# A recurrence with a mixture of experts behind it: second bias, slot stores, loads and steps rearranged in layer 0

## The chip, the cores and the metric

The kernel runs on one core of one Trainium2 chip. The metric is the device time of one execution in microseconds (us). Three timed runs and one profiled execution of the kernel before are at hand; the profile also gives each instruction's start and end on the five engines (PE is TensorE, DVE is VectorE, ACT is ScalarE, POOL is GpSimd, SP is the queue engine that issues loads), the DMA transfers, and the TensorE clock that was granted.

## The reference

The input x has 8 sequences of 512 tokens of width 256, all in float32. Two layers follow one another. Only layer 0 is touched by the change:

```python
h = layernorm(x) * (1 + ca) + sa
# attention: 16 heads of width 16, a delta rule along the tokens
q, k = l2_normalize(silu(h @ Wq.T)), l2_normalize(silu(h @ Wk.T))
v, beta = silu(h @ Wv.T), sigmoid(h @ Wbeta.T)
for t in range(512):                       # M is 16x16 for each sequence and head
    out_t = q_t @ M
    delta = v_t - M @ k_t
    M = M + beta_t * outer(k_t, delta)
x = x + ga * ((out / rms(out)) * rms_weight) @ Wo.T
h = layernorm(x) * (1 + cb) + sb
# experts: each token goes to the one of 8 experts with the largest gate logit
for e in range(8):
    y = relu(h @ w1[e] + b1[e]) @ w2[e] + b2[e]     # 256 -> 1024 -> 256
    out = out + (top_idx == e) * y
x = x + gb * out
```

Layer 1 is softmax attention with a relative position bias and a dense mixture of eight 256x256 experts. Its code is the same before and after.

## The kernel before, in words

Layer 0 takes the 512 tokens as four tiles of 128 tokens, i = 0 to 3; each tile holds the 128 tokens of all 8 sequences (b = 0 to 7). The recurrence of a tile is `scan(i)`: 128 steps on VectorE, each of six instructions (L760 to L794: the products with the key, their sum, the update and the next delta). Its state M is 128x256 and is carried from tile to tile, so the four scans can only follow one another. They run from 56 to 1007 us of the profiled execution.

Everything else of layer 0 is cut into *pieces*. A piece is a function with a number, the step of the scan behind which it is to be issued. The loop that places them is this:

```python
for s, step in enumerate(steps or ()):
    while left and left[0][0] <= s:
        with tc.issue_after(step):
            left.pop(0)[1]()
```

The numbers set the program order. The framework's scheduler then orders the instructions of each engine by their estimated times within what `issue_after` and the buffers allow. During `scan(i)` the pieces are:

- `front(i + 1)`: the next tile's normalized Q, K, V. For each pair p of sequences, `stats(p)` issues the load of `xt` (two buffers) on SP and has ScalarE sum it and take the deviation `sda` (L525); `normal(p)` has VectorE invert it (`rsa`, L541, L542). For each sequence b, `turn`, `project` and `squares` run on ScalarE, TensorE and GpSimd, then `roots` and `scales` normalize; `heads` lays out K and V for the next scan. The front begins at step 47 (for tile 1 at step 30). After the last load SP writes zeros over the slot array `hs_d`.
- `follow(i - 1)`: what comes after the recurrence of the tile before. Its `attend` computes the attention output of that tile from Q, K and the deltas on TensorE: for each sequence `turn`, `scores`, `mask` (`pair`, L891), `weigh` (L924 is the new part of the state), `state` (`dm`, L970; `bdM`, L967), `project`; then `roots` (`ms`, L974), `rest` (adds the output to `x1`) and `stats` of the second layernorm. Its pieces lie on steps 0 to about 65. Then `route` picks the experts and forms the slots.
- `experts(i - 1)`: the tile's 1024 tokens are scattered by an indirect DMA of GpSimd into 15 slots of 128 rows, each slot with one expert. For each slot j SP loads its rows `hslot`, GpSimd fetches the expert's weights by two indirect DMAs (`w0` 128x2056 and `w1` 128x2304, two buffers each; L1192), TensorE multiplies twice (L1238 and L1259) with ScalarE's activation between (L1247), and the sum `py` gets the second bias and is stored to `ys_d`:

```python
nc.scalar.copy(ysb, py[:, :D])
nc.gpsimd.tensor_add(ysb, ysb, w[:, NFC * D :])
nc.gpsimd.dma_start(rows, ysb)
```

 The fetch of `w0` for slot j + 2 is issued behind these on GpSimd. The last slot of the last tile is the exception: VectorE adds the bias to `py`, and SP stores it. Of tiles 0 and 1, eleven slots are issued during the scan and four during the next; of tile 2, twelve during scan 3 and three behind it; of tile 3, all behind it.
- the gathers: when a tile's slots are stored, GpSimd gathers the rows back (L1284), multiplies them by the gates (L1319) and adds them to x in memory by an accumulating DMA (L1320). Those of tile 2 fall behind the scans, between the slots of tile 3. For tile 3 VectorE multiplies.

Behind the scans come `attend(3)`, its routing, the last slots and the gathers, up to about 1270 us. Layer 1 begins at 1287 us.

Of the kernel before, what the change touches and what calls it, by code (L numbers as in the profile page):

```python
# [19 lines left out]
P = 128  # L20
B = 8
S = 512
D = 256
# [41 lines left out]
def tile_two_layers(ctx: ExitStack, tc: tile.TileContext, t: dict, out: bass.AP):  # L65
# [223 lines left out]
    with ExitStack() as l0:  # L289
# [183 lines left out]
        def front(i, at):  # L473
# [27 lines left out]
                    zero.unsqueeze(1).to_broadcast([P, 2 * NSLOT, P]),  # L501
                )

            def stats(p):
                xt = ep.tile([P, 2, D], F32, tag="xt", name=f"xt{i}_{p}", bufs=2)
                load = nc.sync.dma_start(
                    xt,
                    t["x"][2 * p : 2 * p + 2, i * P : (i + 1) * P, :].rearrange("b p d -> p b d"),
                )
                mv = ep.tile([P, 2, 2], F32, tag="mva", name=f"mva{i}_{p}", bufs=2)  # L510
# [13 lines left out]
                sd = ep.tile([P, 2], F32, tag="sda", name=f"sda{i}_{p}")  # L524
                nc.scalar.activation(sd, mv[:, :, 1], AF.Sqrt, bias=ln_eps, scale=1.0 / D)  # L525
                got[p] = xt, mv, sd
                if p == B // 2 - 1:

                    with tc.issue_after(load.ins):
                        nc.sync.dma_start(  # L530
                            hs_d[i].rearrange("(p j) (c d) -> p (j c) d", p=P, c=2),
                            zero.unsqueeze(1).to_broadcast([P, 2 * NSLOT, P]),
                        )

            def normal(p):
                xt, mv, sd = got[p]
# [179 lines left out]
            if i == 0:  # L716
                pieces.append((0, stats_first))
                for b in range(B):
                    pieces.append((4 * b + 4, lambda b=b: turn_first(b)))

                    pieces.append((4 * b + 9, lambda b=b: project_first(b)))
                    pieces.append((4 * b + 13, lambda b=b: squares_first(b)))
                    later.append((1 + 2 * b, lambda b=b: project_q(b)))
                    later.append((4 + 2 * b, lambda b=b: squares_q(b)))
                pieces += [(46, roots_first), (47, scales_first)]
                later += [(22, roots_q), (25, scales_q)]
            else:
                for b in range(B):
                    p, c = divmod(b, 2)
                    if c == 0:  # L730
                        pieces.append((at + 8 * p, lambda p=p: stats(p)))
                        pieces.append((at + 8 * p + 6, lambda p=p: normal(p)))
                    pieces.append((at + 8 * p + 3 * c + 6, lambda b=b: turn(b)))
                    pieces.append((at + 8 * p + 3 * c + 7, lambda b=b: project(b)))
                    pieces.append((at + 8 * p + 3 * c + 13, lambda b=b: squares(b)))
                for h in range(B // n):

                    last = at + 16 * h + 32
                    pieces.append((last, lambda h=h: roots(h)))
                    pieces.append((last + 2, lambda h=h: scales(h)))  # L740
            turns = at + (55 if i else 48)
            pieces.append((turns, lambda: heads("K", qk[:, 1], 1.0)))
            pieces.append((turns + 3, lambda: heads("V", v, -1.0)))
            got["qk"] = qk
# [61 lines left out]
        def attend(i, qk, V, x1, norms):  # L806
# [166 lines left out]
            def roots(h):  # L973
                nc.vector.reciprocal(got["ms", h], got["ms", h])  # L974
# [207 lines left out]
        def experts(i, slot, idx, scatter):  # L1182
# [46 lines left out]
            for j in range(NSLOT):  # L1229
# [34 lines left out]
                rows = ys_d[i][j * P : (j + 1) * P, :]  # L1264
                if (i, j) == (NT - 1, NSLOT - 1):

                    nc.vector.tensor_add(ysb, py[:, :D], w[:, NFC * D :])
                    nc.sync.dma_start(rows, ysb)
                else:
                    nc.scalar.copy(ysb, py[:, :D])  # L1270
                    nc.gpsimd.tensor_add(ysb, ysb, w[:, NFC * D :])
                    nc.gpsimd.dma_start(rows, ysb)
# [36 lines left out]
            for b in range(B + DEPTH[i]):  # L1309
                if b < B:  # L1310

                    room = w1["fetched" if i < NT - 2 else "rows"]
                    yr = room[:, b * D : (b + 1) * D]
                    with tc.issue_after(issued["fetch"]):
                        gather(b, yr)
                    queue.append(yr)
                if b >= DEPTH[i]:
                    yr, k = queue.pop(0), b - DEPTH[i]
                    nc.gpsimd.tensor_mul(yr, yr, gates[1][:, k, :])  # L1319
                    nc.gpsimd.dma_start(x2d[k][i], yr, accum_op=ALU.add)  # L1320
                yield

# [103 lines left out]
        for i in range(NT):  # L1426
# [450 lines left out]
```

## Time and profile before

| | |
|---|---|
| three timed runs | 2044.92, 2048.03, 2048.41 us, median 2048.03 |
| profiled execution | 2056.27 us, span 2054.6 us |
| mean granted TensorE clock | 0.896 |
| busy: PE, DVE, ACT, POOL | 1659.3, 1526.3, 1072.4, 639.2 us |
| scans 0 to 3 | 56.0 to 276.7, 278.7 to 518.8, 520.7 to 778.9, 780.9 to 1007.3 us |
| 16 bare steps of the recurrence | 26.3 us |
| layer 1 | 1287 us to the end |

In the profile, L12 is line 12 of the kernel. A group is named `out<-in` by the program's names. The slices cut the span into 40 pieces of 51.4 us, and each digit is a share in tenths. A wait is put down to the instruction that released it last. Durations come from the profiled execution, which took 8.2 us more than the median of the timed runs.

### The profile page before, as it was taken

To read this page: it belongs to the slowest core of one execution; us is meant where nothing else is said; L and a number is where in the kernel's file an instruction comes from. 1 tells how busy PE (TensorE), PEld (TensorE's weight loads), DVE (VectorE), ACT (ScalarE), POOL (GpSimd) and SP (SyncE) were. 2 spreads that over 40 slices of the span, in tenths; PEclk is the share of its full clock that TensorE was granted. 3 is DMA by queue.
4 is the path that set the end of the run, shared out by engine and by line. 5 is a ranking of instruction groups with operands and counts; after the bars stand their busy time and mean duration, and the time that the engine had idled before them with its cause. 6 is when DMAs were issued, how large, how long until landed. Compare 5 with 4: busy or idle time off the path is not lost. (4 is left out here: it accounts for less than half of the span.)

```text
span 2054.6 us, 33919 instructions
## 1 busy us (share of the span) xinstructions
PE 1659.3 (81%) x11394; PEld 1188.7 (58%) x11394; DVE 1526.3 (74%) x5576; ACT 1072.4 (52%) x2610; POOL 639.2 (31%) x920
## 2 busy tenths in 40 slices
PE   5433147479895898939898988999999999999998
PEld 4211135369774697739766877565555556565553
DVE  4999999989989699899653001787676767676755
ACT  4353135565565755613343334987666675766630
POOL 1223023365462554623365644010111111020121
PEclk8666576699997899969998999999999999999999
DMA  5110000268202583118874973100100010010011
GB/s 178 52 49 11 0 1 11 75 233 320 77 20 78 217 304 138 46 63 312 276 124 119 323 265 105 35 17 9 29 14 25 17 24 16 22 22 11 17 21 18
DMA packets 88783, 189.71 MB, mean 92 GB/s; under 512 B 13713, under 2 KB 67281, under 8 KB 75809
## 3 DMA queue, kind: packets, MB, share of 16 engines
q0 software_dynamic: 33648, 137.30, 20.9%
q1 hardware_dynamic: 54960, 50.24, 8.5%
q8 instruction: 90, 1.47, 0.3%
q14 instruction: 85, 0.69, 0.1%
HBM read 175.12 MB, written 36.93 MB: 103 GB/s over the span
## 5 line engine op out<-in xcount | busy, mean ns | idle before, releaser
L1525 ACT ACTIVATE pr<-pr,low 128x256 f32<-128x256 f32 (+3 forms) x512 | 251.5, 554 | 127.4 <-DVE low L1513 127.0
L1238 PE MATMUL ps<-hTs,w 128*128 128x128 f32 x1920 | 240.7, 287 | 15.1 <-DMA w<-in_wrows,idx 11.9
L1513 DVE CUSTOM_DVE_ANT_0 pr<-ps,strips 128x256 f32<-128x256 f32 (+3 forms) x512 | 219.3, 485 | 42.8 <-PE ps L1500 41.9
L1238 PEld LDWEIGHTS ps<-hTs,w 128*128 128x128 f32 x1920 | 236.3, 202 | 24.0 <-issue 17.0
L1685 PE MATMUL ps<-ew,hTd 128*128 128x512 f32 x512 | 246.2, 608 | 0.0
L1259 PE MATMUL ps<-w,act 128*128 128x256 f32 x960 | 223.6, 387 | 15.5 <-ACT act L1247 10.6
L785 DVE TENSOR_REDUCE sums<-terms 128x17 f32<-128x289 f32 x508 | 226.9, 447 | 2.6 <-DVE upd L776 2.6
L790 DVE TENSOR_TENSOR state<-state,upd 128x256 f32<-128x256 f32 x511 | 214.9, 420 | 0.3 <-DVE sums L785 0.3
L760 DVE TENSOR_TENSOR terms<-state,K 128x256 f32<-128x256 f32 x512 | 211.0, 413 | 1.1 <-DVE kept L794 0.5
L1247 ACT ACTIVATE act<-ps,w 128x128 f32<-128x128 f32 x480 | 137.0, 371 | 140.1 <-PE ps L1238 113.8
L776 DVE TENSOR_TENSOR upd<-K,kept 128x256 f32<-128x256 f32 x511 | 208.8, 409 | 0.0
L1259 PEld LDWEIGHTS ps<-w,act 128*128 128x128 f32 x960 | 181.1, 194 | 41.9 <-ACT act L1247 13.4
L1690 DVE SCALAR_TENSOR_TENSOR accd<-ps,wtd,accd 128x256 f32<-128x256 f32 x256 | 123.2, 481 | 75.2 <-PE ps L1685 66.4
L1538 PEld LDWEIGHTS ps<-cst,pr 128*128 128x128 f32 x1280 | 146.1, 144 | 42.0 <-issue 28.7
L1538 PE MATMUL ps<-cst,pr 128*128 128x128 f32 x1280 | 162.7, 278 | 1.6 <-DVE low L1513 1.1
L1695 POOL TENSOR_TENSOR accd<-accd,bc_g 128x256 f32<-128x256 f32 x28 | 20.3, 724 | 448.2 <-DVE accd L1690 441.0
L1192 POOL DMA_INDIRECT w<-in_wrows,idx x120 | 123.6, 1030 | 100.4 <-ACT hTs L1216 38.7
L1685 PEld LDWEIGHTS ps<-ew,hTd 128*128 128x128 f32 x512 | 89.2, 191 | 98.2 <-issue 75.8
L794 DVE SCALAR_TENSOR_TENSOR kept<-kept,sums 128x16 f32<-128x16 f32 x508 | 117.2, 231 | 0.6 <-DVE state L790 0.6
L1546 DVE COPY prT<-ps 128x384 f32<-128x384 f32 (+1 forms) x192 | 110.2, 592 | 5.0 <-PE ps L1538 4.4
L1500 PE MATMUL ps<-kT,qTc 32*128 32x128 f32 (+3 forms) x1024 | 106.1, 470 | 5.4 <-ACT prT L1544 2.3
L1544 ACT COPY prT<-ps 128x384 f32<-128x384 f32 (+1 forms) x192 | 92.1, 507 | 18.6 <-PE ps L1538 17.3
(303 smaller groups left out, 3090.1 us busy)
## 6 DMA issues: line engine op xcount, KB each, us to landing
hs<-zero SPq DMA_DIRECT2D x4, 1920.0 KB
hslot<-hs SPq DMA_DIRECT2D x60, 128.0 KB
ys<-ysb POOLq DMA_DIRECT2D x59, 128.0 KB
x<-in_x SPq DMA_DIRECT2D x32, 128.0 KB
strips<-strip_d SPq DMA_DIRECT2D x16, 256.0 KB
out<-accd POOLq DMA_DIRECT2D x32, 128.0 KB
wm<-in_wmod SPq DMA_DIRECT2D x4, 768.0 KB
xt<-in_x SPq DMA_DIRECT2D x12, 256.0 KB
```

The costliest lines, as they stand in the source:

```text
L760: nc.vector.tensor_mul(term[:, :HD, :HD], M, K[:, s, :].unsqueeze(1).to_broadcast([P, HD, HD]))
L776: nc.vector.tensor_mul(upd, K[:, s, :].unsqueeze(2).to_broadcast([P, HD, HD]), delta(s).unsqueeze(1).to_broadcast([P, HD, HD]),)
L785: nc.vector.tensor_reduce(sums, term, AX.X, ALU.add)
L790: done = nc.vector.tensor_sub(M, M, upd)
L1192: issued["fetch"] = nc.gpsimd.indirect_dma_start(out=w, out_offset=None, in_=t[f"wrows{part}"], in_offset=bass.IndirectOffsetOnAxis(ap=idx ...
L1238: nc.tensor.matmul(ph[:, q * P : (q + 1) * P], w[:, k * FF + f * P : k * FF + (f + 1) * P], hT[:, k, :], start=(k == 0), stop=(k == 1),)
L1247: nc.scalar.activation(act[:, f, :], ph[:, q * P : (q + 1) * P], AF.Relu, bias=w[:, 2 * FF + f : 2 * FF + f + 1],)
L1259: nc.tensor.matmul(py[:, :D], act[:, f, :], w[:, f * D : (f + 1) * D], start=(f == 0), stop=(f == NFC - 1),)
L1513: nc.vector.tensor_tensor_reduce(out=pr[:, at[i]], in0=pscs[r][:, at[i]], in1=strips[:, n, S - (i + 1) * P :], scale=1.0, scalar=3.0e38, o ...
L1525: nc.scalar.activation(pr, pr, AF.Exp, bias=low, scale=-1.0)
L1538: made = nc.tensor.transpose(pt[:, n * P : (n + 1) * P], prs[r, i][:, j * P : (j + 1) * P], ident)
L1685: nc.tensor.matmul(pe, hT[0][:, k, cols], ew[:, k, e : e + 2, :], start=(k == 0), stop=(k == 1),)
```

## The change

It has four parts. (1) In `experts`, the slots issued during the scans (42) get the second bias by one more matmul into `py`, with a row of ones as the stationary operand and one row of the bias as the moving one; ScalarE still copies `py`. In the slots behind the scans (18, one of them as before) VectorE adds the bias while it reads `py`, without ScalarE's copy. GpSimd's add goes away in all of them, and all slots are stored from SP's queue. (2) `stats` is split: `load(p)` issues the load of `xt` four steps earlier than `stats(p)`, for p = 1 ten steps, and the zeros are written behind the last load. (3) In `front` of tiles 1 to 3, all steps from `normal` on come two steps later. In `attend`, `state`, `roots`, `rest` and `stats` move by one or two steps. (4) The gate product of tile 2's gathers is made by VectorE.

Instructions on each engine's list, before and after: PE 4442 and 4485, DVE 5476 and 5498, ACT 2034 and 1993, POOL 844 and 708, SP 212 and 272.

```diff
-            def stats(p):
-                xt = ep.tile([P, 2, D], F32, tag="xt", name=f"xt{i}_{p}", bufs=2)
-                load = nc.sync.dma_start(
+            def load(p):
+                xt = got[p] = ep.tile([P, 2, D], F32, tag="xt", name=f"xt{i}_{p}", bufs=2)
+                entry = nc.sync.dma_start(
...
+                if p == B // 2 - 1:
+
+                    with tc.issue_after(entry.ins):
+                        nc.sync.dma_start(hs_d[i]..., zero...)
+
+            def stats(p):
+                xt = got[p]
...
                     if c == 0:
+                        ahead = 4 if p != 1 else 10
+                        pieces.append((at + 8 * p - ahead, lambda p=p: load(p)))
                         pieces.append((at + 8 * p, lambda p=p: stats(p)))
-                        pieces.append((at + 8 * p + 6, lambda p=p: normal(p)))
-                    pieces.append((at + 8 * p + 3 * c + 6, lambda b=b: turn(b)))
-                    pieces.append((at + 8 * p + 3 * c + 7, lambda b=b: project(b)))
-                    pieces.append((at + 8 * p + 3 * c + 13, lambda b=b: squares(b)))
+                        pieces.append((at + 8 * p + 8, lambda p=p: normal(p)))
+                    pieces.append((at + 8 * p + 3 * c + 8, lambda b=b: turn(b)))
+                    pieces.append((at + 8 * p + 3 * c + 9, lambda b=b: project(b)))
+                    pieces.append((at + 8 * p + 3 * c + 15, lambda b=b: squares(b)))
...
-                    last = at + 16 * h + 32
+                    last = at + 16 * h + 34
...
-            turns = at + (55 if i else 48)
+            turns = at + (57 if i else 48)
...
                 if i < NT - 1:
-                    pieces.append((4 * b + 12, lambda b=b: state(b)))
+                    pieces.append((4 * b + 13, lambda b=b: state(b)))
...
-                pieces.append((16 * h + 25, lambda h=h: roots(h)))
+                pieces.append((16 * h + 27, lambda h=h: roots(h)))
                 for b in range(4 * h, 4 * h + 4):
-                    pieces.append((13 * h + 25 + b, lambda b=b: rest(b)))
-                    pieces.append((12 * h + 30 + b, lambda b=b: stats(b)))
+                    pieces.append((13 * h + 27 + b, lambda b=b: rest(b)))
+                    pieces.append((12 * h + 31 + b, lambda b=b: stats(b)))
...
                 py = bank()
+                after = "scanned" in issued
                 for f in range(NFC):
                     nc.tensor.matmul(
                         py[:, :D], act[:, f, :], w[:, f * D : (f + 1) * D],
-                        start=(f == 0), stop=(f == NFC - 1),
+                        start=(f == 0), stop=(after and f == NFC - 1),
                     )
...
-                if (i, j) == (NT - 1, NSLOT - 1):
-
+                if after:
                     nc.vector.tensor_add(ysb, py[:, :D], w[:, NFC * D :])
-                    nc.sync.dma_start(rows, ysb)
                 else:
+                    nc.tensor.matmul(
+                        py[:, :D], cst[:1, C_ONES : C_ONES + P], w[:1, NFC * D :],
+                        start=False, stop=True,
+                    )
                     nc.scalar.copy(ysb, py[:, :D])
-                    nc.gpsimd.tensor_add(ysb, ysb, w[:, NFC * D :])
-                    nc.gpsimd.dma_start(rows, ysb)
+                nc.sync.dma_start(ys_d[i][j * P : (j + 1) * P, :], ysb)
...
-                    nc.gpsimd.tensor_mul(yr, yr, gates[1][:, k, :])
+                    (nc.vector if i == NT - 2 else nc.gpsimd).tensor_mul(
+                        yr, yr, gates[1][:, k, :]
+                    )
...
             run(pieces, scan(i, before["K"], before["V"]))
+        issued["scanned"] = True
```

More of the change, by code (lines that the diff above doesn't have):

```diff
@@ L509, in stats @@
                 )
+                if p == B // 2 - 1:
+                    with tc.issue_after(entry.ins):
+                        nc.sync.dma_start(
+                            hs_d[i].rearrange("(p j) (c d) -> p (j c) d", p=P, c=2),
+                            zero.unsqueeze(1).to_broadcast([P, 2 * NSLOT, P]),
+                        )
+            def stats(p):
+                xt = got[p]
                 mv = ep.tile([P, 2, 2], F32, tag="mva", name=f"mva{i}_{p}", bufs=2)
@@ L526, in stats @@
                 got[p] = xt, mv, sd
[L527 to L533, printed above, removed]
             def normal(p):
@@ L1260, in experts @@
                         py[:, :D], act[:, f, :], w[:, f * D : (f + 1) * D],
-                        start=(f == 0), stop=(f == NFC - 1),
+                        start=(f == 0), stop=(after and f == NFC - 1),
                     )
                 ysb = fp.tile([P, D], F32, tag="ysb", name=f"ysb{i}_{j}", bufs=2)
-                rows = ys_d[i][j * P : (j + 1) * P, :]
-                if (i, j) == (NT - 1, NSLOT - 1):
+                if after:
                     nc.vector.tensor_add(ysb, py[:, :D], w[:, NFC * D :])
-                    nc.sync.dma_start(rows, ysb)
                 else:
+                    nc.tensor.matmul(
+                        py[:, :D], cst[:1, C_ONES : C_ONES + P], w[:1, NFC * D :],
+                        start=False, stop=True,
+                    )
                     nc.scalar.copy(ysb, py[:, :D])
-                    nc.gpsimd.tensor_add(ysb, ysb, w[:, NFC * D :])
-                    nc.gpsimd.dma_start(rows, ysb)
+                nc.sync.dma_start(ys_d[i][j * P : (j + 1) * P, :], ysb)
                 if j != NSLOT - 3:
@@ L1318, in experts @@
                     yr, k = queue.pop(0), b - DEPTH[i]
-                    nc.gpsimd.tensor_mul(yr, yr, gates[1][:, k, :])
+                    (nc.vector if i == NT - 2 else nc.gpsimd).tensor_mul(
+                        yr, yr, gates[1][:, k, :]
+                    )
                     nc.gpsimd.dma_start(x2d[k][i], yr, accum_op=ALU.add)
```

## The prediction

> **What bounds the kernel now.** I read the 40 slices first, to find the stages, then the busy time of each engine in those stages, then VectorE's waits there, and last the tail of layer 0.
>
> ```profile
> PE   5433147479895898939898988999999999999998
> ...
> DVE  4999999989989699899653001787676767676755
> ...
> POOL 1223023365462554623365644010111111020121
> PEclk8666576699997899969998999999999999999999
> ```
> ```profile
> 60.00:330.00 270.00, 97.67 (x614) 65.67 (x614) 264.88 (x1019) 96.63 (x227) 66.65 (x135) 0.67 0.08 23
> 330.00:600.00 270.00, 216.88 (x1488) 175.20 (x1485) 246.10 (x953) 152.02 (x408) 131.93 (x202) 0.84 0.38 138
> 600.00:865.00 265.00, 223.35 (x1608) 184.02 (x1607) 232.62 (x902) 154.98 (x422) 130.43 (x197) 0.91 0.42 148
> ```
>
> The columns of the second are stretch, length, then busy time of PE, PEld, DVE, ACT, POOL, then granted clock, DMA share and GB/s. From about 56 to 1007 us the four scans run and VectorE sets the time: 265 of 270 us busy at first, then 246 of 270 and 233 of 265. What is missing is VectorE waiting, about 60 us between 60 and 1008. Layer 1, from 1287 us, is not touched. The waits of VectorE between 60 and 1200 us (line, what it waits for, total, times, longest) say for whom:
>
> ```profile
> DVE rsa L541 <- ACT sda L525: 35.0, 7, 17.4
> DVE pair L891 <- ACT dtok L827: 22.3, 1, 22.3
> ...
> DVE dm L970 <- PE ps L924: 10.2, 6, 4.1
> DVE ms L974 <- ACT ms L959: 9.1, 6, 3.0
> DVE bdM L967 <- PE ps L924: 3.0, 1, 3.0
> ```
>
> 35.0 us go to `normal` of the next tile, which asks for the deviation `sda` before ScalarE has it; 22.3 us to `attend` of the tile that is running (10.2 + 9.1 + 3.0). The 22.3 us of `pair` are after the last scan: there VectorE waits for TensorE, which still has tile 2's slots in front of it.
>
> After 1120 us VectorE is idle and tile 3's fifteen slots set the time:
>
> ```profile
> 1120.00:1160.00 40.00, 38.00 (x248) 35.14 (x249) 4.11 (x6) 15.96 (x55) 24.86 (x30) 0.96 0.86 304
> 1160.00:1190.00 30.00, 22.30 (x148) 19.80 (x147) 2.17 (x8) 8.08 (x28) 21.82 (x25) 0.99 0.97 312
> 1190.00:1232.00 42.00, 37.20 (x218) 33.81 (x217) 0.00 (x0) 13.84 (x48) 16.88 (x20) 0.89 0.74 251
> 1232.00:1265.00 33.00, 32.45 (x217) 29.99 (x217) 1.31 (x4) 13.88 (x46) 11.39 (x14) 1.00 0.35 114
> ```
> ```profile
> L1271 POOL TENSOR_TENSOR ysb<-ysb,w 128x256 f32<-128x256 f32 x59 | 43.1, 730 | 169.9 <-ACT ysb L1270 169.8
> L1272 POOL DMA_DIRECT2D ys<-ysb x59 | 35.6, 604 | 9.0 <-POOL ysb L1271 8.9
> ```
>
> TensorE is idle 2.0, 7.7, 4.8 and 0.6 us in the four, 15 us together. The chain of waits there runs over POOL: the add L1271, the store L1272, the gathers L1284 and the fetches L1192 stand in it one behind another. The two groups (busy, mean ns, then idle before) show what POOL spends on the second bias and the stores, and that it stands 170 us waiting for ScalarE's copy with its fetches behind it.
>
> **The change, part by part.**
>
> *1. `normal` and all of the front two steps later, loads earlier.* A bare step of the recurrence takes 26.3 us / 16 = 1.644 us, so VectorE asks 3.29 us later. The seven waits, read one by one, are 0.36 and 4.61 in scan 0; 2.47 and 6.10 in scan 1; 2.47, 1.60 and 17.36 in scan 2. Each falls by up to 3.29: 3.65 + 5.76 + 7.36 = 16.8 us. The largest needs a second look. ScalarE executes `sda` of the last pair behind the copy of tile 0's slot 14; it is idle for 9.1 us before that copy, waiting for the slot's sum, while the scatter of tile 1 (655.6 to 665.6 us) is on the DMA engines. The order after the change has slot 14's activation sooner, but the first slot's activation of tile 1 still stands ahead of `sda`. Between nothing and 9.1 I take half: 16.8 + 4.5 = **−21** (16 to 26, and to 35 if all of it goes). The earlier loads are costed at nothing: the loads of the first pair are short (0.38 us median, 4.9 at most) and already land before ScalarE is free. Should a load be later in line behind a slot's store on SP, the cost is one store, below 2 us. Later heads for K and V are hidden too: they are done at about 502 and 761 us, with the scans ending at 519 and 779, so 16 us of cover against 3.3. Without it the next scan would start 3.3 us late, twice.
>
> *2. `attend`: state one step later, roots and rest two.* Taken wait by wait, dm and bdM could fall by 1.64 us each (9.1 us over seven) and ms by all 9.1: −18. But between 540 and 600 and between 800 and 865 us TensorE is busy 57.4 of 60 and 62.3 of 65 us: VectorE follows TensorE's pace there, and a later request wins its offset once for each tile, not at each of the eight batches. Three tiles by 1.64 to 3.29 us give 5 to 10: **−7**. The gap between `rest` and `stats` becomes one step shorter, so VectorE may meet POOL's sum of x1 unfinished; POOL is relieved of 1.33 us for each slot, so I put +1 us on each of three tiles: **+3** (0 to +8).
>
> *3. The second bias as a K=1 matmul, in the 42 slots issued under the scans.* It adds two rows of 128x256 for each slot. No row of the trace has one contracted row at this width. The nearest is L1259, where 16 rows take 3.46 us: 0.216 each, so 0.43 us a slot, and 0.86 at half clock. The other end would be nothing, since only one row of the array carries data. Here the Trainium skill, "TensorE: Matmul & The Clock Gate", section "Step-by-step: what each phase is for", speaks against the change: it gives the time as purely that of the N columns streamed, however few rows are contracted. So I take the full 0.43; 42 x 0.43 = 18.1 us of TensorE. In scans 1 and 2 it lies beside VectorE: TensorE has 53 and 42 us free in the two windows, against 15 x 0.43 = 6.5. In scan 3 it does not. There tile 2's slots run from 925.5 to 1026.8 us, beyond the scan's end, and `pair` waits for that: 12 x 0.43 = +5.2. On the same stretch the removed POOL add frees POOL 3.5 us earlier for the fetch two slots ahead, and the waits for weights (1.1 + 3.6 us, and the half clock behind them) may go: −7. Together **−2** (+5 to −8).
>
> *4. Behind the scans: VectorE adds from PSUM, no POOL add, stores on SP, gate products of tile 2 on VectorE.* Eighteen slots lie here, and one already worked so. The added VectorE work (17 + 8 instructions of 0.4 to 0.7 us) is hidden by an engine with 7.6 us busy in 145; with it busy it would cost about 0.5 us for a slot, 7 us. POOL's list for a slot in the first eight is add 0.72, store 0.60, gather 1.0, product 0.74, two fetches 1.03 each, accumulate 1.0: 6.1, and 7.5 with the gaps, above TensorE's 7.25. After: 4.1, about 5.2 with gaps. Then TensorE or the transfers set the pace. If POOL alone made the idle time, 15 us go. Against that stands a row: between 1160 and 1190 us the DMA share is 0.97 at 312 GB/s. The Trainium skill's opening page, "Trainium Kernel Development and Optimization", section "Key Constraints", says that DMAs of all queues run on the same 16 engines and that several queues save only issue time; by the rule the store's move wins nothing where the transfers are full, and the 7.7 us stay: 2.0 + 4.8 = −7. By the row alone, fetches issued 3.5 us sooner fill the less busy stretches on both sides (0.86 and 0.74). I take half of the 7.7: **−10** (−15 to −3). POOL still waits at each accumulate for a product, now VectorE's, with fetches behind it; that wait for the gather's landing is not new.
>
> *Sum.* −21 − 7 + 3 − 2 − 10 = −37 us. Against the profiled execution, 2056.27 us (span 2054.6), that gives 2019. The median of the runs shown is 8.2 lower, 2048.03, so the forecast is **2011 us**.
>
> **The rivals.** A measurement of this kernel can tell about 0.2%, 4.1 us, from no change.
>
> *A (0.50): as above, 2011 us.*
>
> *B (0.22): the waits move.* ScalarE's order decides, not the request's step. `sda` comes later by as much as the request does, because ScalarE still has the slots' activations ahead of it and the early loads only find their two buffers taken; in that sense the change does not do what it says. For it: the 17.36 us wait is a matter of order. Against: the shorter ones (1.6 to 6.1 us) are of the size of two steps. The scans then win about 8 (half of the six short waits, 17.6 us) and nothing in `attend`; the tail wins 7, scan 3's end gives 1 back: −14, 2034 us.
>
> *C (0.13): everything goes.* 35 + 18 in the scans, 15 in the tail, less the 5 for matmuls: −63, 1985 us.
>
> *D (0.15): slower, TensorE becomes the bound of the scans.* With the K=1 matmuls TensorE falls behind and VectorE waits for `dm` and for the next tile's Q, K, V instead of `sda`. It decides once the 6.5 us for each tile (13 at half clock) no longer fit into TensorE's idle stretches. For it: TensorE is 95% busy in 925 to 1008 us (78.8 of 83), and the granted clock is 0.67 to 0.91 in the scans. Against: it is idle 20 of the 80 us between 640 and 720, where the longest wait lies. If all 18.1 us land on the path and nothing is won in the scans, the tail's −10 leaves +8.1: 2056 us.
>
> **How the numbers follow.** Faster by over 0.2% (below 2043.9) are A, C and 0.19 of B: 0.82. Slower (above 2052.1) is 0.13 of D. The rest, 0.03 of B and 0.02 of D, is 0.05. C's lower half and D are left out of the range: from 1984 to 2046.
>
> **What would show it.** Right: the `sda` waits total under 15 us, the 17.4 is under 10, `dm` and `ms` together under 14; scan 3's last step ends 20 to 35 us earlier; POOL has no row for `ysb`; tile 3's last slot ends about 10 us sooner relative to its first; TensorE's idle between 1190 and 1232 has gone. Wrong: a new wait of VectorE on POOL's x1 or on PE of over 10 us; `pair` waiting over 25 us at the last scan's end (the K=1 matmuls on the path); SP's transfer of `hslot` landing later behind a store; the tail's DMA share at 0.97 over a longer stretch with TensorE as idle as before.

## The result: 22 us slower

The changed kernel takes 2067.99 us (median of six runs, 2062.12 to 2072.02) against 2046.48 us for six runs of the kernel before: a ratio of 1.0111, 95% interval 1.0086 to 1.0137. The forecast was 2011 us, with a range of 1984 to 2046. The profiled execution of the changed kernel took 2068.29 us, span 2066.5, granted clock 0.896 as before.

These are the slices of the changed kernel's page, answering to those shown before:

```profile
PE   5433055589896798967998988999999999999998
...
DVE  4999999889688797899944112787676867676755
...
POOL 1223024243253532623254433010111111020121
PEclk8666577699997998978997999899999999999999
```

GpSimd is relieved where it was meant to be, and VectorE still has its dips in the scans. The same windows as before (columns: stretch, length, busy PE, PEld, DVE, ACT, POOL, clock, DMA share, GB/s):

```profile
60.00:330.00 270.00, 99.36 (x657) 66.24 (x657) 269.85 (x1038) 95.03 (x231) 69.25 (x140) 0.69 0.08 23
330.00:600.00 270.00, 214.74 (x1371) 168.48 (x1369) 231.58 (x898) 141.41 (x373) 105.28 (x160) 0.85 0.39 138
600.00:865.00 265.00, 230.25 (x1539) 182.37 (x1540) 224.95 (x873) 152.06 (x408) 108.40 (x165) 0.90 0.42 146
```

VectorE is busier in the first window (269.9 us against 264.9), where the wait of 4.6 us has gone, and less busy in the next two (231.6 against 246.1, 225.0 against 232.6). Its waits between 60 and 1220 us say on whom:

```profile
DVE dm L975 <- PE ps L929: 40.3, 13, 10.3
DVE rows L1325 <- DMA rows<-ys,slot: 31.7, 6, 8.5
DVE ysb L1271 <- PE ps L1265: 29.3, 6, 7.8
DVE rsa L544 <- ACT sda L535: 19.8, 2, 11.1
DVE pair L896 <- ACT dtok L832: 16.2, 1, 16.2
...
DVE over L1139 <- PE ps L1131: 10.5, 3, 4.7
```

The `sda` waits fell from 35.0 to 19.8 us, but they are now two waits instead of seven. `dm`, VectorE's wait for TensorE in `attend`, rose from 10.2 to 40.3, and `over`, a wait for TensorE in the router, is new in the scans. (The two groups `rows` and `ysb` lie behind the scans, where VectorE has long idle stretches.) The table gives the milestones of one profiled execution each, from the first and last instructions of the pieces:

| us | before | before, second profile | changed |
|---|---|---|---|
| length of scans 0 to 3 | 220, 240, 258, 226 | 220, 237, 250, 230 | 215, 242, 264, 242 |
| end of scan 3 | 1006.9 | 998.1 | 1026.6 |
| period of a slot in scans 1, 2, 3 (median of six) | 7.46, 7.25, 7.71 | 7.43, 7.25, 7.52 | 8.07, 8.07, 8.07 |
| tile 3: first slot starts, last ends | 1131.9, 1264.9 | 1115.8, 1253.8 | 1146.4, 1271.4 |

Scan 0 wins 5 us, the others lose, and tile 3's slots take 125 us instead of 133 or 138. The second profile of before is one of the experiments. It shows that the profile on which the sum was built was a long one in the scans: scan 3 ended 9 us later in it than in the second. A difference of less than 9 us between two single profiles is therefore no evidence by itself; the ratios below rest on several executions each.

What a slot costs now can be read from TensorE. The first row below is the second layer's matmul, the second the added one (groups by shape between 300 and 1130 us); the other two are waits of the weight loads between 930 and 1040 us.

```profile
L1265 PE MATMUL ps<-w,act 128*128 128x256 f32 x698 | 163.2, 388 | 1.0 <-ACT hTs L1221 0.9
L1273 PE MATMUL ps<-w,cst 1*128 1x256 f32 x84 | 29.2, 426 | 0.0
```
```profile
PEld ps L1273 <- issue: 4.0, 12, 0.3
PEld ps L1243 <- issue: 3.7, 11, 0.3
```

The mean durations, 426 and 388 ns, look alike, because a row's duration includes its overlap with the next. The waits tell more: once in every slot the weight load of the one-row matmul stands still for 0.3 us, and once more the first load of the next 128-row matmul behind it. From the start of a slot's last L1265 matmul to the start of the next slot's first L1243 it takes 0.93 us.

### The profile page after: what moved, and what is told of

Same layout as the page of the kernel before. It is cut to its first block, busy times and chain, and to the rows that moved or that the text cites. A ratio compares the mean times of both kernels' runs of the same rounds, so it can differ in the third digit from the quotient of the medians.

```text
span 2066.5 us, 34057 instructions
## 1 busy us (share of the span) xinstructions
PE 1693.9 (82%) x11478; PEld 1200.6 (58%) x11478; DVE 1532.9 (74%) x5601; ACT 1066.0 (52%) x2589; POOL 554.7 (27%) x794
## 3 DMA queue, kind: packets, MB, share of 16 engines
q0 software_dynamic: 30816, 129.57, 19.6%
## 4 chain that ended last, share of the span: by engine, by line
PE 58%; DVE 21%; ACT 6%; DMA 6%; issue 5%; POOL 3%; SPq 0%; POOLq 0%; ACTq 0%; DVEq 0%
PE ps L1243 9%; PE ps L1694 9%; PE ps L1265 8%; PE ps L1547 6%; PE ps L1509 4%; DVE sums L790 4%; PE ps L1570 3%; DVE state L795 3%; DVE upd L781 3%; DVE terms L765 3%; PE ps L257 2%; DVE kept L799 1%; DMA strips<-strip_d 1%; PE ps L241 1%; PE ps L1623 1%
## 5 line engine op out<-in xcount | busy, mean ns | idle before, releaser
L1243 PE MATMUL ps<-hTs,w 128*128 128x128 f32 x1920 | 241.9, 287 | 9.3 <-DVE ysb L1271 4.7
L1243 PEld LDWEIGHTS ps<-hTs,w 128*128 128x128 f32 x1920 | 233.6, 201 | 22.1 <-issue 11.2
L1265 PE MATMUL ps<-w,act 128*128 128x256 f32 x960 | 225.0, 389 | 9.0 <-ACT act L1252 7.9
L1265 PEld LDWEIGHTS ps<-w,act 128*128 128x128 f32 x960 | 183.1, 196 | 34.1 <-ACT act L1252 8.1
L1553 ACT COPY prT<-ps 128x384 f32<-128x384 f32 (+1 forms) x192 | 92.2, 507 | 19.9 <-PE ps L1547 18.5
```

What stands on the lines that cost most here:

```text
L1243: nc.tensor.matmul(ph[:, q * P : (q + 1) * P], w[:, k * FF + f * P : k * FF + (f + 1) * P], hT[:, k, :], start=(k == 0), stop=(k == 1),)
L1265: nc.tensor.matmul(py[:, :D], act[:, f, :], w[:, f * D : (f + 1) * D], start=(f == 0), stop=(after and f == NFC - 1),)
```

## The experiments

Ratios are to runs of the kernel before on the same chip, with 95% intervals. 1% is 20 us. Two families: the changed kernel with one part undone, and the kernel before with one part alone.

### The price of the matmul

Without any second bias under the scans:

```diff
-                    nc.tensor.matmul(
-                        py[:, :D], cst[:1, C_ONES : C_ONES + P], w[:1, NFC * D :],
-                        start=False, stop=True,
-                    )
                     nc.scalar.copy(ysb, py[:, :D])
```

> The changed kernel without the one-row matmul: the 42 slots issued under the scans get no second bias at all, everything else as changed. Theory P (the matmul's price is the cause: it takes about 0.83 us a slot where 0.43 was counted, and TensorE carries the delay of each scan's eleven or twelve slots into the next attend): the period of a slot under the scans falls from 8.08 to 7.25 us, scan 3 ends at least 20 us sooner (before 1006 us instead of 1026.6), VectorE's waits for dm fall from 40 to under 15 us, and the time is 2035 to 2048 us, 20 to 30 below the changed kernel. Theory Q (the later steps of front and attend are the cause): the slots get quicker but the scans still end at 1015 us or later, and the time stays above 2055.

Measured: ratio 0.9964 (0.9945 to 0.9984), so 1.5% or 30 us below the changed kernel. Period 7.25 to 7.27, scan 3 ends at 1012.1, `dm` waits for 25.8 us. The time is as theory P said; the waits in the scans fell less (scan 3's end was expected before 1006, `dm` under 15), so a part of the loss is not the matmul's.

The same matmul over 128 rows:

```diff
-                        py[:, :D], cst[:1, C_ONES : C_ONES + P], w[:1, NFC * D :],
+                        py[:, :D], ident, w[:, NFC * D :],
```

> The changed kernel with the bias matmul made over all 128 rows: the identity is the stationary operand and all rows of the bias (which are equal) the moving one. The number of columns streamed is the same. Theory P with the price in the change of the row count (128 to 1 and back, with the weights not loaded ahead): the period of a slot falls from 8.08 to about 7.68 us, 0.43 above the bare 7.25, and the time by 11 to 15 us to about 2055. Theory P with the price in the added matmul as such: the period stays at 8.08 and the time at 2068. Theory Q: the time stays within 5 us of 2068 whatever the period does.

Measured: 1.0023 (1.0003 to 1.0043), 2054.28 us. The period is 7.68 in all three scans. The group and the interval between the same two matmuls as above:

```profile
L1273 PE MATMUL ps<-w,cst 128*128 128x256 f32 x84 | 25.0, 379 | 0.0
```

No wait of a weight load on "issue" is left in this stretch, and the interval is 0.65 us instead of 0.93 (0.22 in the kernel without the matmul), in every slot where nothing else stands between. The rest of the saving lies just behind it: the next slot's first L1243 matmul is followed by its second after 0.11 us instead of 0.21. So a bias row that is 128 times larger is 0.39 us a slot cheaper (8.07 − 7.68), and 42 × 0.39 = 16 us is about what the ratios differ by (0.0088, 18 us). The added matmul as such costs the 0.43 us that the prediction counted (7.68 − 7.25); the other half of the price is the change of row count.

The matmul alone in the kernel before:

```diff
+                    if not after:
+                        nc.tensor.matmul(
+                            py[:, :D], cst[:1, C_ONES : C_ONES + P], w[:1, NFC * D :],
+                            start=False, stop=True,
+                        )
                     nc.scalar.copy(ysb, py[:, :D])
-                    nc.gpsimd.tensor_add(ysb, ysb, w[:, NFC * D :])
+                    if after:
+                        nc.gpsimd.tensor_add(ysb, ysb, w[:, NFC * D :])
```

> The kernel before with the one-row matmul alone in the slots under the scans (no add on GpSimd there; GpSimd still stores). Theory P: period 8.08, waits for dm above 25 us, time 2066 to 2076 us. Theory Q: 2044 to 2054 us.

Measured: 1.0100 (1.0065 to 1.0134), 2067.28 us, period 8.07. This edit alone costs 20 us, nearly as much as the whole change; the other parts of the change, below, largely cancel one another. The waits of VectorE between 60 and 1000 us:

```profile
DVE rsa L541 <- ACT sda L525: 29.4, 5, 13.8
DVE dm L970 <- PE ps L924: 27.6, 6, 6.7
```

`dm` is 27.6 us, where the second profile of before has 12.5. The way from slot to wait is in the trace: slot 10 of the tile ends 1 us after the next scan's start in that profile of before (517.0 against 516.1) 7 us after it here (527.1 against 520.4) and 12 us after it in the changed kernel (530.6 against 518.6). `attend` stands behind it on TensorE, fills TensorE (in the changed kernel 58.4 of the 60 us from 560 to 620), and VectorE meets `dm` late.

GpSimd's add in its place, in the changed kernel:

```diff
-                    nc.tensor.matmul(
-                        py[:, :D], cst[:1, C_ONES : C_ONES + P], w[:1, NFC * D :],
-                        start=False, stop=True,
-                    )
                     nc.scalar.copy(ysb, py[:, :D])
+                    nc.gpsimd.tensor_add(ysb, ysb, w[:, NFC * D :])
```

> The changed kernel with the one-row matmul replaced, under the scans, by what was there before: ScalarE copies and GpSimd adds the bias; the store stays on SP and all steps stay as changed. It differs from the kernel without any bias under the scans only by 42 adds of 0.72 us on GpSimd. If GpSimd's add was free under the scans: 2042 to 2048 us where before takes 2048 (ratio 0.995 to 1.000), periods of 7.25 us. If the add delays the fetches two slots ahead, the periods are 7.3 to 7.5 and the ratio is 1.002 to 1.008.

Measured: 0.9976 (0.9955 to 0.9996), period 7.25 in scans 2 and 3, 7.57 in scan 1. This overlaps with the kernel without any bias: the add on GpSimd that the change removed under the scans costs nothing that shows, and the matmul in its place costs 1.35%, 28 us.

### The later steps

All later steps and the early loads, on the kernel before (the diff of `front`, `attend` and `load` as in the change, the rest as before):

> The kernel before with the loads split off and all the later steps (front and attend), and nothing of the bias, the stores or the gate products. Theory R (with its eleven slots, the attend and the next front on it, TensorE's own chain sets how soon a tile is through; a later request only turns VectorE's wait for sda into a wait for dm and for the router's over): scan 0 gets about 5 us shorter, scans 1 to 3 do not; sda waits fall from 35 to about 15 to 20 us, dm rises from 10 to 20 or more, over from 0 to about 9; the sum of VectorE's waits in the scans stays within 10 us of 59, and the time within 5 us of before (2045 to 2055). Theory W (the later steps win what the prediction said, 18 us, and only the matmul took it back): waits below 45 us, time 2028 to 2040.

Measured: 1.0040 (1.0024 to 1.0055), 2050.78 us: slower by 8 us, a little more than theory R allowed, and far from W.

```profile
DVE rsa L544 <- ACT sda L535: 20.2, 2, 11.1
DVE dm L975 <- PE ps L929: 20.1, 12, 5.9
DVE over L1139 <- PE ps L1131: 8.6, 2, 4.4
DVE ms L979 <- ACT ms L964: 5.4, 2, 2.7
```

The sum of VectorE's waits for others in the scans is 58.2 us; it was 56.2 and 51.5 in the two profiles of before. What `sda` no longer takes, `dm` and `over` take.

`attend`'s later steps alone:

```diff
-                    pieces.append((4 * b + 12, lambda b=b: state(b)))
+                    pieces.append((4 * b + 13, lambda b=b: state(b)))
...
-                pieces.append((16 * h + 25, lambda h=h: roots(h)))
+                pieces.append((16 * h + 27, lambda h=h: roots(h)))
-                    pieces.append((13 * h + 25 + b, lambda b=b: rest(b)))
-                    pieces.append((12 * h + 30 + b, lambda b=b: stats(b)))
+                    pieces.append((13 * h + 27 + b, lambda b=b: rest(b)))
+                    pieces.append((12 * h + 31 + b, lambda b=b: stats(b)))
```

> The kernel before with attend's later steps alone (state, roots, rest, stats). Theory R: over appears with about 4 us for a tile, ms and dm do not fall by more than 3 us together, time 0 to +8 against before. Theory W: -5 to -8.

Measured: 0.9981 (0.9957 to 1.0004). Unclear by itself, at −4 us between the two theories. `ms` falls from 8.0 us (second profile of before) to 5.4, and `dm` rises from 12.5 to 18.4. No `over` appears; that expectation was wrong.

`front`'s later steps and the loads alone:

> The kernel before with the loads and front's later steps alone. Theory R: scan 0 5 us shorter, sda waits 15 us less, of which dm takes about 10 back: -2 to -8 against before. Theory W: -15 or more.

Measured: 1.0050 (1.0029 to 1.0071), 2053.37 us: slower by 10 us, where both theories had it faster. Scan 0 is 5 us shorter as expected (215.2 against 219.6), but scan 1 is 245.1 us long against 236.9.

```profile
DVE rsa L544 <- ACT sda L535: 18.7, 2, 10.0
...
DVE over L1139 <- PE ps L1131: 7.9, 2, 4.7
...
DVE count L1124 <- PE ps L1119: 3.4, 2, 1.9
```

Two things are to be seen. `over` and `count` belong to the router. Its small matmuls stand behind a projection of the next tile on TensorE; between 378 and 397 us:

```profile
L562 PE MATMUL ps<-wqkv,hT 128*128 128x512 f32 x8 | 7.6, 1099 | 3.5 <-ACT hT L146 3.5
```

They stand behind it in the kernel before too, but there the last four matmuls of this projection take 1.98 us and not 3.78, and VectorE finds `over` done. The granted clock (third number from the right) differs between 390 and 400 us; the first row is this run, the other the second profile of before:

```profile
390.00:400.00 10.00, 7.05 (x17) 4.04 (x17) 5.33 (x28) 3.79 (x10) 3.24 (x8) 0.67 0.00 0
390.00:400.00 10.00, 5.61 (x19) 3.36 (x20) 7.53 (x36) 8.99 (x23) 3.88 (x9) 0.96 0.07 16
```

Why the clock was lower here is not shown.

The other thing is that the two remaining `sda` waits, both of a tile's fourth pair, are no shorter: 8.6 and 10.0 us against 4.7 and 12.3. The early loads did not come early. There are two `xt` buffers, and from the third load on each load is issued within 0.1 us of the end of the last `xna` of the pair two before (one of them 0.9 us after it), in the kernel before as in this one; a later `turn` therefore makes the load later.

But VectorE does not wait for the load: the fourth pairs' loads are issued at 399.0 and 654.3 us, and ScalarE first reads those pairs at 428.0 and 682.9, over 28 us later. ScalarE works in order, and ahead of these reads stands the copy `hTs` of the scan's first slot, for which it waits 6.8 and 4.6 us because the slot's rows have not landed. That copy starts 19.9 and 21.9 us after the first issue of the scatter; in the second profile of before it is 17.2 and 17.4.

The zeros for `hs_d` are written behind the last load, so they became later with it: 1920 KB at 654.7 us, on top of the scatter that begins at 653.6, where in the second profile of before they went at 644.1, six us ahead of it. In all six kernels with `front`'s later steps and all loads, the copy starts 19.6 us or more after the scatter (up to 23.0). In the nine profiles with the zeros ahead of the scatter it is 17.0 to 17.6 us in 12 of 18 cases, but the first profile of before has 19.6 and 24.7, so the zeros are not the only thing that can delay it.

The second profile of before:

> The kernel before once more, unchanged, for a second profile of it. Scan 0's end, scan 3's end and tile 3's last slot should lie within 5 us of 276, 1007 and 1265; if tile 3's slots take clearly under 133 us here, part of the difference to the changed kernel's 125 is scatter of single executions.

Measured: 2047.39 us, span 2045.7. Scan 3's end lies 9 and tile 3's last slot 11 us sooner than in the first profile, more than was expected, and tile 3's slots take 138 us, more rather than less.

The third and fourth pair not loaded, with `front`'s later steps:

```diff
             def load(p):
+                if p < 2:
...
+                    got["xt", p] = xt
+                got[p] = got["xt", p % 2]
```

> The kernel before with the loads and front's later steps alone, and the third and fourth pair of each of tiles 1 to 3 not loaded: their layernorm reads the first and second pair's x again, so no load waits for one of the two xt buffers to come free. Theory B (the load of a pair is issued 0.6 us after the last use of the pair two before, so a later turn makes the load and sda later too, and the request only runs ahead of itself): the sda waits, 18.7 us with the loads, fall below 6 us; dm takes part of it back; the time is 4 to 12 us below that kernel's 2053 against 2044 before, so a ratio of 0.998 to 1.003. Theory A (ScalarE's order behind the activations holds sda back): sda waits stay above 14 us and the ratio at 1.005.

Measured: 0.9970 (0.9949 to 0.9992), 0.8% or 16 us below the same steps with the loads, and faster than either theory said. `sda` waits are 9.7 us (18.7), between the two, and `over` stays:

```profile
DVE dm L978 <- PE ps L932: 14.4, 6, 4.0
DVE rsa L547 <- ACT sda L538: 9.7, 2, 5.6
DVE over L1142 <- PE ps L1134: 8.0, 2, 4.7
```

The run was meant to test the buffers, but it also moves the zeros: they now follow the second pair's load, a scan earlier. The first 12.5 us from the start of tile 1's scatter, with the later steps and then with these loads left out (the last two numbers are DMA share and GB/s):

```profile
653.50:666.00 12.50, 8.04 (x33) 5.57 (x32) 12.50 (x50) 10.12 (x27) 9.68 (x10) 0.97 0.88 261
650.50:663.00 12.50, 8.04 (x33) 5.57 (x32) 12.50 (x50) 10.11 (x27) 9.67 (x10) 0.97 0.28 91
```

The scatter's DMAs land 2.4 us after their issue (median) and not 6.6, TensorE's wait for the first slot's rows falls from 5.0 to 0.2 us, and the copy `hTs` starts 16.9 and 17.1 us after the scatter's first issue. As ScalarE read these pairs only 28 us after their loads were issued, the traces point to the zeros, and not to the buffers as such, for the half of the wait that went. This is not shown: no run moves the zeros alone. In the other half `sda` still stands in order behind the slot's activations on ScalarE.

The same with the steps as before:

> The kernel before with the loads split off and early, the steps as before, and the third and fourth pair not loaded, as in the run beside it. Theory B: sda waits under 8 us (27 to 35 before) with no wait for the router's over, ratio 0.992 to 0.998. Theory A: sda waits above 20 us, ratio 0.999 to 1.001.

Measured: 0.9982 (0.9962 to 1.0002), `sda` waits 28.0 us. Theory A holds for the kernel before: neither the loads nor their buffers are what VectorE waits for, and the zeros, ahead of the scatter before as well, matter little there.

### The part behind the scans, and the stores

The part behind the scans alone (VectorE adds and SP stores there, VectorE's gate products for tile 2):

> The kernel before with the part behind the scans alone: VectorE adds the bias there, SP stores, VectorE makes tile 2's gate products. Both theories: the fifteen slots of tile 3 take about 125 us instead of 133, and the time falls by 6 to 10 us, to 2036 to 2042. If the gain is taken back by the gathers or by layer 1's start, less than 3 us.

Measured: 1.0001 (0.9983 to 1.0018): nothing. In the profile tile 3's slots take 125.7 us, as expected, but they start late: from the end of tile 2's slot 11 to tile 3's first slot it takes 106.0 us, against 97.9 and 105.1 in the two profiles of before. Between 1104 and 1128 us, in tile 2's last slots, TensorE waits for VectorE's add to give a bank back:

```profile
PE ps L1238 <- DVE ysb L1267: 2.5, 1, 2.5
```

In the changed kernel that wait is 4.7 us. As the two profiles of before are 7 us apart here, it is not shown that this is all of what was given back.

The stores on SP, alone:

```diff
-                    nc.gpsimd.dma_start(rows, ysb)
+                    nc.sync.dma_start(rows, ysb)
```

> The kernel before with one edit: the 59 stores of the slots go to SP's queue; GpSimd still adds the bias, everything else as before. If the stores are what held the fetches of tile 2's slots back in scan 3 (7.5 to 8 us a slot in the profiles of before, 7.25 in the mix): period 7.25 in scan 3 and a ratio of 0.992 to 0.997. If the gain of the mix (0.990) needs attend's steps or the part behind the scans: 0.998 to 1.001.

Measured: 0.9927 (0.9900 to 0.9954), 2032.33 us: one line wins 15 us. The period is 7.25 in all scans. The same window of tile 2's slots, 930 to 990 us, in the second profile of before and then with the stores on SP:

```profile
930.00:990.00 60.00, 57.31 (x388) 52.83 (x387) 60.00 (x233) 22.31 (x77) 25.25 (x31) 1.00 0.86 312
```
```profile
930.00:990.00 60.00, 60.00 (x415) 56.56 (x414) 60.00 (x235) 23.68 (x81) 22.06 (x26) 1.00 0.95 341
```

TensorE has no idle left, and the transfers run at 341 GB/s where they ran at 312. Tile 2's twelve slots in scan 3 take 91.2 us from the first one's start to the last one's end, where the two profiles of before have 101.3 and 101.4; the slots in scans 1 and 2 take as long as before (100.0 and 98.5 us for eleven, 99.8 and 100.0 in the second profile of before). GpSimd's fetches are issued earlier:

```profile
POOL w L1192 <- ACT hTs L1216: 37.5, 12, 8.8
POOL ysb L1271 <- ACT ysb L1270: 22.7, 12, 3.3
```
```profile
POOL ysb L1271 <- ACT ysb L1270: 47.2, 12, 9.2
POOL w L1192 <- ACT hTs L1216: 14.6, 4, 10.0
```

The first two are with the stores on SP, the others before (900 to 1030 us). GpSimd now spends its waiting time at the fetches, ready to issue, and half as much at the add.

`attend`'s steps, all stores on SP, and the part behind the scans together; `front` and the bias under the scans as before:

> The parts that cost nothing, together: the kernel before with attend's later steps, every slot stored from SP, and behind the scans VectorE's add and gate products; under the scans ScalarE copies and GpSimd adds as before, front and the loads are as before. If SP's stores under the scans free GpSimd: ratio 0.990 to 0.997. If neither the stores nor the steps matter: 0.997 to 1.001.

Measured: 0.9901 (0.9873 to 0.9929), 2026.38 us, faster than both kernels.

The same without `attend`'s steps:

> The mix without attend's later steps: all stores on SP, and VectorE's add and gate products behind the scans. If attend's steps win about 0.2% as they did alone: 0.991 to 0.994 against the mix's 0.990. If they do nothing: 0.989 to 0.991. The part behind the scans gave nothing with its stores alone moved (1.0001); if it gives something only once GpSimd stores nowhere, this run lies 0.003 or more below the run with the stores alone.

Measured: 0.9931 (0.9906 to 0.9956). So the part behind the scans adds nothing to the stores (0.9927), and `attend`'s steps win 0.3%; the intervals overlap, so that is likely rather than shown.

The mix with `front` two steps later for tile 1 only:

```diff
+            lag = 2 if i == 1 else 0
...
-                        pieces.append((at + 8 * p + 6, lambda p=p: normal(p)))
+                        pieces.append((at + 8 * p + 6 + lag, lambda p=p: normal(p)))
```

> The mix, with front's two later steps for tile 1 only (scan 0, where no attend and no router stand in the way), loads as before. Scan 0 should be 5 us shorter and the later scans as in the mix: ratio 0.987 to 0.989 against its 0.990. If a shorter scan 0 only brings the waits forward into scan 1: 0.990.

Measured: 0.9892 (0.9862 to 0.9922), 2026.75 us. Scan 0 is 214.7 us long, 5 us less; as a whole it can't be told from the mix. This and the mix are the best versions seen, 1% below before and 2% below the changed kernel.

## Why the prediction was wrong

Put together in one order, the runs divide the change as follows. The mix stands at −20 us. `front`'s later steps and the loads on top of it cost +15 (0.9901 to 0.9976), and the matmul in place of GpSimd's add on top of that +28 (0.9976 to 1.0111). That these give the measured +22 but for rounding is no check, since each is the difference to the next ratio. Nor do the parts simply add: alone on the kernel before, `front` and the loads cost +10 and the matmul +20. Against the forecast, two steps are off by some 30 us each: step 3 (−2 forecast, +28 measured) and step 1 (−21, and +10 to +15). Step 3 turned the sign: with the add in the matmul's place the same kernel is faster than before (0.9976).

*Step 3, the matmul: a step that failed, in size and in cover.* The size: 0.43 us a slot was counted, from the nearest row; it is 0.82 (8.07 − 7.25), and 42 slots make 34 us of TensorE and not 18. The nearest row had 128 rows beside 128-row neighbours, and what costs the other half is that one row stands between 128-row ones. The page that the prediction weighed counts the columns streamed; that holds for the matmul over 128 rows (0.43 as counted), and not for the single row between others. The Trainium skill, "TensorEngine Tiling (Array Packing)", section "Key Properties", says that changing the tiling mode drains TensorE. If one row counts as another mode, the 0.3 us twice in each slot, gone with 128 rows, agree with it; no run here separates a drain from a weight load that is not taken ahead.

The cover: in scans 1 and 2 the matmuls were put "beside VectorE" because TensorE had 53 and 42 us free in the windows. Most of that idle time lies before the slots begin (at 421 us in scan 1), as three narrower windows of the same profile show (after the length, the first number is TensorE's busy time):

```profile
330.00:421.00 91.00, 48.36 (x209) 31.98 (x205) 81.07 (x327) 48.37 (x123) 33.67 (x53) 0.61 0.24 79
421.00:440.00 19.00, 18.67 (x105) 15.93 (x106) 12.90 (x52) 14.74 (x42) 7.59 (x15) 0.90 0.64 234
440.00:520.00 80.00, 77.38 (x511) 70.06 (x510) 79.89 (x305) 42.35 (x120) 46.26 (x66) 1.00 0.79 292
```

TensorE is idle for 43 us in the first of them, and for 3 us in the two others together. The slots run almost without a gap up to the end of the scan and over it, with the next `attend` behind them. A mean over a window hid it; the end of slot 10 against the start of the next scan (521.5 and 520.7) would have shown that there was no cover. Eleven slots take 111.4 and 107.2 us in scans 1 and 2 of the changed kernel, where they took 100.2 and 99.6. In scan 3, the only place where the prediction charged for the matmul, its −2 came about: the twelve slots take 97.6 us instead of 101.3. But the −7 in it was put down to the removed add, and it was the store: with the add kept and the stores on SP they take 92.9 us, with no bias at all 93.1.

*Step 1, `front` and the loads: the other step that failed.* The 3.65 us of scan 0 came, and a bit more (5). In scans 1 and 2 the sum moved VectorE's request and left `sda` where it was. But the fourth pair's `sda` became later too: counted from the start of scan 1 it is ready after 161.6 us with `front`'s steps alone, and after 156.7 and 153.9 in the two profiles of before (in scan 2 after 169.2, against 174.3 and 166.6). It stands in order on ScalarE behind the first slot's copy, and the zeros that follow the last load had moved onto the scatter which that slot waits for. Two waits, 18.7 us together, remain, and `over` and `count` (11.3 us) and `dm` took the rest. The loads were costed from a misread row: 0.38 us is the time of a load's issue on SP, over all twelve loads, and not that of its landing. Rival B had named ScalarE's order and "their two buffers taken", and both are there; neither it nor the prediction looked at the zeros, nor at the router's matmuls. As these differences come from single profiles, only the time (+10 alone, clear of noise) is shown; its division among these causes is read from the traces.

*Step 2, `attend`: −7 + 3 predicted, about −4 to −6 measured.* The size came, within an interval that touches zero. The reasoning that TensorE's pace limits it held: what `ms` lost, `dm` took. (One of the six `ms` waits that were counted, 1.0 us, lies behind the last scan.)

*Step 4, behind the scans: −10 predicted, nothing measured for VectorE's part.* Tile 3's slots were 8 us quicker in the changed kernel, as counted; they started later. What was worth the most was counted least: the store's move, which gained most under scan 3. The prediction's row, 312 GB/s at a DMA share of 0.97, did not show full transfers: in the stretch that answers to it, 28 us behind tile 3's first slot, the kernel with all stores on SP reaches 360 GB/s (1135 to 1165 us). In the changed kernel, though, TensorE is idle there for 7.9 us (1174 to 1204 us, 327 GB/s) where it was 7.7, as the rule had it; the gain came from two slots behind it, 7.2 us each instead of 11.7 and 10.2.

*The rivals.* D, that TensorE becomes the bound of the scans, is what happened, by its own point of decision: 0.82 a slot no longer fits. It was given 0.15, and its price of +8 was too small because it took over the 0.43 and set `front` at nothing, where it cost 10 to 15 us.

## What to carry to other kernels

Before a matmul is added "beside" another engine, look at when its engine finishes the chain, not at how idle it is on average: if its last piece ends where the next stage wants it, what is added can go on the path. Keep the row count of neighbouring matmuls the same; an identity over 128 rows was half the price of one row of ones. When a request is moved later to hide a wait, follow what the late work frees (buffers), what is issued behind that (here a load, and behind it 1920 KB of zeros) and what it then meets; and try the cheapest edit alone, since here one line gained 15 us that the others hid.

## What was not expected of the hardware

A one-row matmul of 256 columns between 128-row ones held TensorE for 0.82 us a slot, a 128-row one with as many columns for 0.43. Between 930 and 990 us, indirect loads from GpSimd's queue and plain stores ran at 341 GB/s together when the stores came from SP, and at 312 when they came from GpSimd. The DMAs of a scatter landed 6.6 us after their issue (median) when 1920 KB of zeros were written beside them, and after 2.4 us without. Two profiled executions of the same kernel were 9 us apart (spans 2054.6 and 2045.7), with single waits of 17.4 and 12.3 us at the same place: a sum over one execution's waits carries that scatter.
